# A four-layer network on one NeuronCore: 16-bit one-hots made ahead in two dispatches, and expert sums, latent pieces, layer-norm statistics and a block bias moved in the program

## Chip, cores and metric

The kernel runs on one core of a Trainium2 chip, in one launch. The metric is the device time of that launch in microseconds (us), the median over runs. Five engines run their own instruction lists, each in order: TensorE (PE; its weight loads are listed as PEld), VectorE (DVE), ScalarE (ACT), GpSimd (POOL) and SyncE (SP). They meet through semaphores. Transfers run on 16 DMA engines and are issued from the lists of SP and POOL.

## What is computed

The activations `x` are 4 sequences of 512 tokens with 256 features. Four layers follow one another. Each normalises `x` and adds an attention part and a feed-forward part, both taken from the same normalised rows:

```python
for layer in (L0, L1, L2, L3):
    xn = layernorm(x)
    x = x + layer.attn(xn) + layer.ffn(xn)

L0.attn: gated projection, then a decaying scan over tokens
L0.ffn : "thought" vector of the last token, 4 residual MLP steps, gated broadcast
L1.attn: dilated attention, 16 heads, segments of 64, every 2nd token
L1.ffn : mixture of 32 experts (width 128), each token goes to its best 4
L2.attn: 16 heads of gated linear attention with 64 memory slots:
         ok = read of keys through the slots, pv = softmax(ok), o = read of values,
         o = rms_norm(o) * g * sigmoid(g), then Wo
L2.ffn : x + causal latent attention (16 heads, rotary half), then a mixture of
         7 routed experts (best 2) and one shared expert (width 128)
L3.attn: causal attention, one head of 256
L3.ffn : mixture of 8 experts (width 512), each token goes to its best 2
```

All of it is float32 in the reference.

## The kernel before

**Data.** `x` lies on the chip as 16 tiles of 128 tokens by 256 features; four tiles are one sequence, called a block here (0 to 3). `xn` holds the normalised rows, `xnT` their transpose. A second use of the word block is a group of 128 picked rows of one expert: that is the unit in which the mixtures of experts are computed.

**Mixtures of experts.** The picks of a layer are sorted by expert into slots (`dispatch` in layers 2 and 3 with 38 and 39 blocks of 128 slots; `places1` in layer 1 with 126). TensorE counts the picks (`count`, `rank`, L213 and L215) and VectorE works out each pick's slot. Then comes the inversion, from slot to token: for each of 16 token tiles and each of its picks (2 in `dispatch`, 4 in `places1`) VectorE makes two one-hots, `place` (L268, 128 x 128, which slot inside a block) and `token` (L270, 128 x blocks, the token's number in the column of its block), and TensorE adds their product into `in_slot` (L273). In layer 3 the one-hots lie in a tile called `pieces`, and by that name they stand in the profile. `in_slot` is the index list of the gathers: `load_rows` (L334) issues an indirect DMA from GpSimd for each expert block's rows; L365 transposes them (`rt`), the expert's products follow, and L374 scatters the results to memory. In layer 1 and layer 3 a count that is only known on the chip selects one of several compiled programs (`Switch`), a branch of all engines. `places1` already has 16-bit one-hots (`lane` L1252, `token` L1254, every fourth `token` on GpSimd) in rings of eight buffers.

**Layer 1.** After the branch, `Line` runs the expert blocks as turns of two, with gathers ahead. `block_bias` (`hot` L1293, `bt` L1295, `bb` L1303) makes the bias of every block from a one-hot of its expert. Sums go back through indirect gathers: `collect1` issues for every token tile four gathers (L1277, into tiles that appear as `xn` and `xnT`) and VectorE adds each to `x` with its weight (L523). The layer norm of block 0 that layer 2 begins with follows (`st` L429, `mv` L430, `rs` L418 and L420 on GpSimd, `xn` L448, then the transposes `tr` L463).

**Layer 2.** Work is written as generators, and each `yield` ends a piece; the order in which pieces are drawn is the program order, and a scheduler keeps each engine's list near to it. 32 units (8 for each block, two heads each) of the linear attention are run by `run(u, beside, rate)`. A unit's steps are a string of 19 letters: `m` is this unit's chain, `s` the supply of the next unit's projections, `d` the drain of the unit before. After each step it adds `rate` to a credit, and draws one piece of a beside-chain for each whole credit:

- units 0 to 23: `latent_chain`, 208 pieces at 0.44 a step; what is left is drawn to its end after unit 23. It has its own norm (`junk`, `rms`, `a`), projections (`kp`, `qp`, `vp`), and for each head a pass that finds the maxima (`qk` L2061, `mx` L2068) and one that computes the values (`kq` L2093, `pr` L2098, `pv` L2109). `qk` and `kq` share a pool of four PSUM buffers.
- units 24 to 29: `routed2`, the dispatch and the routed experts, at 1.45 a step;
- unit 30: `ended2` at 0.75: the expert sums (`collect`: two plain loads for each pair of token tiles, a GpSimd addition L390, a VectorE addition to `x` L392), the norm of block 0 for layer 3 and its routing;
- unit 31: `ahead3`, norms and routing of blocks 1 and 2.

In units 0 to 5 the steps with `n % 8 != 7` also draw from `collects`, the layer-1 sums of blocks 1 to 3, five tiles deep. `issue_after` keeps an instruction's place in its engine's list behind a marked one. In the chain of a unit the names that matter are `eF` (L1677, L1678), `turn` (L1698), `ke` (L1720, L1722), `sc`/`s` (L1730, L1736), `pok`/`ok`/`okt` (L1763, L1774, L1778), `pov` (L1809) and `o` (L1858).

**Layer 3.** TensorE's order is written out: groups of `in_slot` products lie between the attention's scores `sc`, the transposes `pt` (L2391), `ov` (L2422) and the output product `o` (L1474). One-hots and their ring of four lie in a weight buffer not yet needed.

Of the kernel before, what the change touches and what calls it, by code (L numbers as in the profile page):

```python
# [14 lines left out]
P = 128  # L15
NB = 4
# [99 lines left out]
class Net:  # L116
    def __init__(self, ctx, tc, a):
# [55 lines left out]
        self.lane = const.tile([P, P], F32, tag="lane", name="lane")  # L173
        nc.gpsimd.iota(self.lane, [[1, P]], base=0, channel_multiplier=0, allow_small_or_imprecise_dtypes=True)
        self.starts = const.tile([P, 96], F32, tag="starts", name="starts")
        nc.gpsimd.iota(self.starts, [[P, 96]], base=0, channel_multiplier=0, allow_small_or_imprecise_dtypes=True)
# [22 lines left out]
    def dispatch(self, moe, rows, top, w, wk, pool, tag, keep=None):  # L199
# [8 lines left out]
        keep = keep or wk  # L208
# [56 lines left out]
        for i in range(NTILE):  # L265
            for m in range(k):
                place = wk.tile([P, P], F32, tag="place", name="place", bufs=4)
                nc.vector.tensor_scalar(place, self.lane, inside[:, i, m : m + 1], None, ALU.is_equal)  # L268
                token = wk.tile([P, blocks], F32, tag="token", name="token", bufs=4)
                nc.vector.tensor_scalar(  # L270
                    token, self.starts[:, :blocks], first[:, i, m : m + 1], less[:, i : i + 1], ALU.is_equal, ALU.mult
                )
                nc.tensor.matmul(  # L273
                    ps, place, token, start=(i == m == 0), stop=(i == NTILE - 1 and m == k - 1)
                )
            if i % 2:
                yield
# [100 lines left out]
    def collect(self, moe, wk, of=range(0, NTILE, 2)):  # L378

        for i in of:  # L380
            x = self.x[:, i : i + 2, :]
            ys = []
            for m in range(moe["k"]):
                y = wk.tile([P, 2, D], F32, tag="sum", name="sum", bufs=8)
                s = (m * NTILE + i) * P
                self.load(y, moe["outs"][s : s + 2 * P, :].rearrange("(n p) d -> p n d", p=P))
                ys.append(y)
            if moe is self.moe2:
                for m in range(len(ys) // 2):
                    self.nc.gpsimd.tensor_tensor(ys[m], ys[m], ys.pop(), ALU.add)  # L390
            for y in ys[1:] + ys[:1]:
                self.nc.vector.tensor_tensor(x, x, y, ALU.add)  # L392
# [434 lines left out]
    def slots1(self, counts, upto, rank, once, go_on, rt):  # L827
# [9 lines left out]
        own = self.starts[:, :ne]  # L837
# [158 lines left out]
    def table1(self, routing):  # L996
# [19 lines left out]
        self.lane16 = routing.tile([P, P], F16, tag="lane16", name="lane16")  # L1016
        nc.gpsimd.tensor_copy(self.lane16, self.lane)
        self.starts16 = routing.tile([P, 126], F16, tag="starts16", name="starts16")
        nc.gpsimd.iota(self.starts16, [[P, 126]], base=0, channel_multiplier=0, allow_small_or_imprecise_dtypes=True)
# [28 lines left out]
    def layer1(self):  # L1048
        nc, a, moe, r1 = self.nc, self.a, self.moe1, self.r1
        with ExitStack() as ctx:  # L1050
# [54 lines left out]
            for pairs in self.arms1(0, [1 + 2 * i for i in range(PAIRS // 2 + 1)]):  # L1105
                line = Line(self)
                self.fetch1(4)
                self.block_bias(bias, wa, ptr, po, (bg, bu1))
# [134 lines left out]
    def places1(self, wk, pool):  # L1243
# [39 lines left out]
    def block_bias(self, bias, wk, ptr, psm, biases):  # L1283
# [9 lines left out]
        nc.vector.tensor_scalar(hot, self.lane[:n, :ne], of, None, ALU.is_equal)  # L1293
# [7 lines left out]
        ps = psm.tile([P, 2, n], F32, tag="o", name="bb")  # L1301
# [179 lines left out]
    def layer2(self):  # L1481
# [8 lines left out]
        with ExitStack() as ctx:  # L1490
# [33 lines left out]
            def run(u, beside, rate):  # L1524
# [18 lines left out]
            collects = {b: self.collect1(b, 5) for b in range(1, NB)}  # L1543
# [21 lines left out]
            run(UNITS - 2, self.ended2(wk, gp["ex"]), 0.75)  # L1565
# [137 lines left out]
    def gated_unit(self, t):  # L1703
# [70 lines left out]
        nc.vector.tensor_tensor(ok, pok, rz, ALU.mult)  # L1774
# [422 lines left out]
    def layer3(self):  # L2197
        nc, a = self.nc, self.a
        with ExitStack() as ctx:
# [9 lines left out]
            with self.tc.manual_schedule(engines={mybir.EngineType.PE}):  # L2209
# [12 lines left out]
                slots = self.dispatch(moe, self.rows, self.top3, self.w3, pieces, psm, "sm", wp)  # L2222
# [304 lines left out]
```

## Time and profile before

| | us |
|---|---|
| median of 3 runs (2184.61, 2185.09, 2187.05) | 2185.09 |
| profiled execution, whole time | 2185.53 |
| its span in the trace | 2183.7 |
| PE busy / share of span | 1960.7 / 90% |
| PEld busy | 1439.0 / 66% |
| DVE busy | 1195.1 / 55% |
| ACT busy | 829.1 / 38% |
| POOL busy | 639.5 / 29% |

The mean granted TensorE clock of the profiled execution is 0.927 of full speed. Line numbers (L268) are those of the kernel before. Where a view gives "idle before" or "waited for", it names the instruction that released the waiting one last. "issue" is a wait that the profile cannot assign. The layers lie about at these places of the span: layers 0 and 1 to about 420 us, layer 2 to about 1830, layer 3 to the end.

### The profile page before, as it was taken

Reading aid. Unit: us, or ns where it says so; the run is one execution under the profiler, and the core shown is the slowest. Engines: PE = TensorE matmul, PEld = TensorE weight load, DVE = VectorE, ACT = ScalarE, POOL = GpSimd, SP = SyncE. Lnnn points to the kernel's source line nnn. Section 1 sums busy time; section 2 is a strip of 40 time slices with the busy share of each in tenths; the row PEclk is TensorE's granted clock in tenths of the full one; section 3 lists DMA queues with packets and bytes.
Section 4 is the critical chain, followed back from the end, with each engine's and each line's share of the span. In section 5 each row is a group of like instructions: output and inputs, shape, how many; then the busy total and the mean of one; then the engine's idle time right before and its main releaser. Section 6 shows DMA issues by size and latency. Waiting matters only on the chain.

```text
span 2183.7 us, 35377 instructions
## 1 busy us (share of the span) xinstructions
PE 1960.7 (90%) x13015; PEld 1439.0 (66%) x13015; DVE 1195.1 (55%) x3451; ACT 829.1 (38%) x1678; POOL 639.5 (29%) x746
## 2 busy tenths in 40 slices
PE   5854998488999999999999999999999979799995
PEld 2522877255666766667666676667787867578895
DVE  5747674486656565555565555546556564413222
ACT  1253344323344443334443343342445434335321
POOL 6334572563211211111211211111454451022231
PEclk9955999678999999999999999987999989899998
DMA  8412885621000000000000000101433220267796
GB/s 289 136 38 82 282 271 155 183 61 32 1 1 9 23 10 6 1 1 8 22 11 6 1 1 8 42 11 47 151 120 111 82 80 1 69 219 263 232 329 234
DMA packets 149549, 198.21 MB, mean 91 GB/s; under 512 B 16885, under 2 KB 127576, under 8 KB 149208
## 3 DMA queue, kind: packets, MB, share of 16 engines
q1 hardware_dynamic: 135224, 156.40, 22.0%
q0 software_dynamic: 14112, 39.15, 6.0%
q8 instruction: 111, 1.82, 0.3%
q14 instruction: 102, 0.84, 0.1%
HBM read 154.21 MB, written 41.29 MB: 90 GB/s over the span
## 4 chain that ended last, share of the span: by engine, by line
PE 56%; DVE 9%; issue 6%; POOL 5%; DMA 4%; ACT 2%; SPq 0%; DVEq 0%; POOLq 0%; ACTq 0%
PE pt L1745 8%; PE pj L1667 6%; PE o L1858 4%; PE g L2278 4%; PE kq L2093 3%; PE sc L1730 3%; PE pov L1809 2%; DVE junk L2068 2%; PE pv L2109 2%; PE qk L2061 2%; PE o L2291 2%; DMA r<-l_rows,in_slot 1%; PE st L1718 1%; PE turn L1698 1%; PE pok L1763 1%
## 5 line engine op out<-in xcount | busy, mean ns | idle before, releaser
L2068 DVE CUSTOM_DVE_ANT_0 junk<-qk,hide 128x512 f32<-128x512 f32 (+3 forms) x256 | 124.5, 486 | 43.6 <-PE qk L2061 25.1
L2101 POOL TENSOR_SCALAR_AFFINE_SELECT pr<-pr 128x512 f32<-128x512 f32 x64 | 40.3, 642 | 341.3 <-ACT pr L2098 341.3
L2278 PEld LDWEIGHTS g<-rT,we 128*128 128x128 f32 x1120 | 132.0, 194 | 5.3 <-ACT rT L367 3.3
L2278 PE MATMUL g<-rT,we 128*128 128x128 f32 x1120 | 132.9, 278 | 1.8 <-ACT rT L367 1.8
L1745 PE MATMUL pt<-Wg,xnT 128*128 128x256 f32 x512 | 126.2, 399 | 2.0 <-ACT h L1630 1.0
L334 POOL DMA_INDIRECT r<-l_rows,in_slot x73 | 72.2, 989 | 189.4 <-PE rt L365 104.9
L374 POOL DMA_INDIRECT l_outs<-y,to x73 | 72.5, 993 | 182.0 <-ACT y L373 148.0
L1745 PE MATMUL pt<-Wv,xnT 128*128 128x256 f32 x512 | 122.4, 391 | 0.0
L1858 PE MATMUL o<-Wo,oT 128*128 128x256 f32 x512 | 122.0, 381 | 0.0
L1736 DVE TENSOR_TENSOR s<-sc,keep 128x512 f32<-128x512 f32 x128 | 82.4, 683 | 67.2 <-PE sc L1730 67.1
L1680 DVE RECIPROCAL rz<-rz 128x128 f32<-128x128 f32 x128 | 116.8, 933 | 0.4
L1745 PEld LDWEIGHTS pt<-Wg,xnT 128*128 128x128 f32 x512 | 98.2, 198 | 27.3 <-issue 6.5
L346 DVE TENSOR_TENSOR mine<-r,number 128x2 f32<-128x2 f32 x73 | 12.8, 175 | 177.0 <-DMA r<-l_rows,in_slot 169.5
L1745 PEld LDWEIGHTS pt<-Wv,xnT 128*128 128x128 f32 x512 | 96.5, 194 | 15.7 <-issue 0.2
L2098 ACT ACTIVATE pr<-kq 128x512 f32<-128x512 f32 (+1 forms) x192 | 86.1, 530 | 48.5 <-PE kq L2093 48.1
L1858 PEld LDWEIGHTS o<-Wo,oT 128*128 128x128 f32 x512 | 96.2, 197 | 8.5 <-issue 0.7
L1313 POOL DMA_INDIRECT r<-l_rows,in_slot x84 | 83.2, 990 | 61.9 <-PE rt L1325 28.1
L2093 PE MATMUL kq<-q,kT 32*128 32x128 f32 (+3 forms) x512 | 87.4, 490 | 7.6 <-DVE mx L2068 5.9
L1748 ACT COPY v<-pt 128x512 f32<-128x512 f32 x64 | 37.5, 586 | 129.2 <-PE pt L1745 129.2
L1826 DVE TENSOR_TENSOR o<-pov,g 128x512 f32<-128x512 f32 x64 | 41.3, 686 | 77.0 <-ACT sq L1825 77.0
L1831 POOL TENSOR_TENSOR rs<-ms,sm 128x8 f32<-128x8 f32 x32 | 6.6, 205 | 243.0 <-DVE ms L1829 242.9
L1825 ACT ACTIVATE sq<-pov 128x512 f32<-128x512 f32 x64 | 34.8, 595 | 102.6 <-PE pov L1815 77.4
(561 smaller groups left out, 4624.2 us busy)
## 6 DMA issues: line engine op xcount, KB each, us to landing
we<-l_w SPq DMA_DIRECT2D x70, 512.0 KB
we<-l_wo SPq DMA_DIRECT2D x35, 512.0 KB
l_outs<-none SPq DMA_DIRECT2D x1, 11776.0 KB
l_outs<-y SPq DMA_DIRECT2D x42, 256.0 KB
we<-l_r_gate SPq DMA_DIRECT2D x38, 128.0 KB
we<-l_r_up SPq DMA_DIRECT2D x38, 128.0 KB
we<-l_r_down SPq DMA_DIRECT2D x38, 128.0 KB
l_rows<-xn SPq DMA_DIRECT2D x8, 544.0 KB
```

Of the source, the lines that this page charges most:

```text
L334: self.nc.gpsimd.indirect_dma_start(out=r[:, m, :], out_offset=None, in_=moe["rows"][:, :], in_offset=bass.IndirectOffsetOnAxis(ap=moe["in ...
L374: self.no_order(moe["name"] + " back", nc.gpsimd.indirect_dma_start(out=moe["outs"][:, :], out_offset=bass.IndirectOffsetOnAxis(ap=to, axi ...
L1313: nc.gpsimd.indirect_dma_start(out=r[:, i, :], out_offset=None, in_=moe["rows"][:, :], in_offset=bass.IndirectOffsetOnAxis(ap=moe["in_slot ...
L1667: nc.tensor.matmul(ps, w[n][:, k, :], self.xnT[:, k, t["b"] * T : (t["b"] + 1) * T], start=(k == 0), stop=(k == KD - 1))
L1680: inverse = lambda c: nc.vector.reciprocal(rz[:, c * P : (c + 1) * P], rz[:, c * P : (c + 1) * P])
L1736: nc.vector.tensor_tensor(s, ps[hh], keep4, ALU.mult)
L1745: nc.tensor.matmul(ps[:, i, :], self.xnT[:, k, s : s + P], w[n][:, k, :], start=(k == 0), stop=(k == KD - 1))
L1858: nc.tensor.matmul(ps[:, p, :], of_parity(oT[:, h, c * D : (c + 1) * D], p), wo[:, h, :], start=(h == 0), stop=(h == 1),)
L2068: nc.vector.tensor_tensor_reduce(out=junk[:, :m], in0=tiles[j][:, off : off + m], in1=self.hide[:, T - m :], op0=ALU.add, op1=ALU.max, sca ...
L2093: nc.tensor.matmul(tiles[j][:, BLOCK[i] - off : BLOCK[i] - off + T - i * P], kT[r, i * P : (i + 1) * P], qT[r, i * P :], start=True, stop= ...
L2098: nc.scalar.activation(pr[:, j, off : off + m], tiles[j][:, :m], AF.Exp, scale=0.25)
L2278: nc.tensor.matmul(pt[:, m, :], we[:, q, k * T + m * P : k * T + (m + 1) * P], rT[:, k, :], start=(k == 0), stop=(k == KD - 1),)
```

## The change

- In `dispatch` the one-hots and the two rows of numbers that they are compared with become 16-bit (`lane16`, `starts16`); the one-hots lie in rings of eight; a tile's products are put two tiles behind its one-hots. In layer 3 the one-hots come from the pool `wk3` (`hots`). `places1` has rings of 12 instead of 8. Layer 1's own uses of the float32 rows get small tiles `own` and `lane32`.
- `block_bias` is called after the second turn instead of before the first, with its two small products in the pool `pd`.
- The statistics of block 0's layer norm are spread between the layer-1 sums, a tile's after the tile's last sum, instead of after all.
- Unit 0 of layer 2 begins with a credit of -8 steps; gathers of later blocks are drawn only after its sixth step, eight tiles deep instead of five.
- `collect` is split into `fetch_rows` (loads) and `add_rows` (additions). `ended2` issues the loads of the first four pairs at once, yields six times, and puts the additions behind `ok` of the unit (`self.late`); its credit is 1.0 a step instead of 0.75.

```diff
@@ -262,17 +262,22 @@
         nc.vector.tensor_tensor(inside, slots, first, ALU.subtract)
         nc.vector.tensor_scalar(less, self.number[:, :NTILE], float(-NB * T), None, ALU.add)
         ps = pool.tile([P, blocks], F32, tag=tag, name="in_slot")
-        for i in range(NTILE):
-            for m in range(k):
-                place = wk.tile([P, P], F32, tag="place", name="place", bufs=4)
-                nc.vector.tensor_scalar(place, self.lane, inside[:, i, m : m + 1], None, ALU.is_equal)
-                token = wk.tile([P, blocks], F32, tag="token", name="token", bufs=4)
-                nc.vector.tensor_scalar(
-                    token, self.starts[:, :blocks], first[:, i, m : m + 1], less[:, i : i + 1], ALU.is_equal, ALU.mult
-                )
-                nc.tensor.matmul(
-                    ps, place, token, start=(i == m == 0), stop=(i == NTILE - 1 and m == k - 1)
-                )
+        ones = []
+        for i in range(NTILE + 2):
+            if i < NTILE:
+                for m in range(k):
+                    place = hots.tile([P, P], F16, tag="place", name="place", bufs=8)
+                    nc.vector.tensor_scalar(place, self.lane16, inside[:, i, m : m + 1], None, ALU.is_equal)
+                    token = hots.tile([P, blocks], F16, tag="token", name="token", bufs=8)
+                    nc.vector.tensor_scalar(
+                        token, self.starts16[:, :blocks], first[:, i, m : m + 1], less[:, i : i + 1], ALU.is_equal, ALU.mult
+                    )
+                    ones.append((place, token))
+            if i > 1:
+                for m in range(k):
+                    nc.tensor.matmul(
+                        ps, *ones[(i - 2) * k + m], start=(i == 2 and m == 0), stop=(i == NTILE + 1 and m == k - 1)
+                    )
             if i % 2:
                 yield
         moe["in_slot"] = in_slot = tile("in_slot", P, blocks, dt=mybir.dt.uint32, of=keep)
...
@@ -378,18 +383,24 @@
     def collect(self, moe, wk, of=range(0, NTILE, 2)):
 
         for i in of:
-            x = self.x[:, i : i + 2, :]
-            ys = []
-            for m in range(moe["k"]):
-                y = wk.tile([P, 2, D], F32, tag="sum", name="sum", bufs=8)
-                s = (m * NTILE + i) * P
-                self.load(y, moe["outs"][s : s + 2 * P, :].rearrange("(n p) d -> p n d", p=P))
-                ys.append(y)
-            if moe is self.moe2:
-                for m in range(len(ys) // 2):
-                    self.nc.gpsimd.tensor_tensor(ys[m], ys[m], ys.pop(), ALU.add)
-            for y in ys[1:] + ys[:1]:
-                self.nc.vector.tensor_tensor(x, x, y, ALU.add)
+            self.add_rows(moe, i, self.fetch_rows(moe, i, wk))
+
+    def fetch_rows(self, moe, i, wk):
+        ys = []
+        for m in range(moe["k"]):
+            y = wk.tile([P, 2, D], F32, tag="sum", name="sum", bufs=8)
+            s = (m * NTILE + i) * P
+            self.load(y, moe["outs"][s : s + 2 * P, :].rearrange("(n p) d -> p n d", p=P))
+            ys.append(y)
+        return ys
+
+    def add_rows(self, moe, i, ys):
+        x = self.x[:, i : i + 2, :]
+        if moe is self.moe2:
+            for m in range(len(ys) // 2):
+                self.nc.gpsimd.tensor_tensor(ys[m], ys[m], ys.pop(), ALU.add)
+        for y in ys[1:] + ys[:1]:
+            self.nc.vector.tensor_tensor(x, x, y, ALU.add)
 
 
 
...
@@ -1105,7 +1116,6 @@
             for pairs in self.arms1(0, [1 + 2 * i for i in range(PAIRS // 2 + 1)]):
                 line = Line(self)
                 self.fetch1(4)
-                self.block_bias(bias, wa, ptr, po, (bg, bu1))
                 at = lambda n: 2 * n if n < STATIC // 2 + pairs else None
                 pieces = self.beside1(bd, wa, ptr, pd, [dilated(u) for u in (2, 3, 4, 5)])
                 credit, rate = 0.0, 35 / (STATIC // 2 + pairs - 1)
...
@@ -1113,6 +1123,8 @@
                     line.turn(
                         dict(t=2 * n, n=n, parts=[static(2 * n), static(2 * n + 1)], done=static_done), at(n + 3)
                     )
+                    if n == 1:
+                        self.block_bias(bias, wa, ptr, pd, (bg, bu1))
                     if n in (8, 10):
                         self.fetch1(singles_at + n - 8, held[n // 2 - 4])
                     credit += rate
...
@@ -1152,10 +1164,20 @@
             last = [dilated(u) for u in (6, 7)]
             next(last[0])
             turns = {1: 0, 4: 0, 5: 1, 8: 1, 10: 0, 12: 1}
+            st, mv = self.stats.tile([P, 4, 6], F32, tag="st", name="st"), self.stats.tile([P, 4, 2], F32, tag="mv", name="mv")
             for n, _ in enumerate(self.collect1(0, 2)):
+                if n > 4 and n % 4 == 1:
+                    i = n // 4 - 1
+                    nc.vector.bn_stats(st[:, i, :], self.x[:, i, :])
+                    nc.vector.bn_aggr(mv[:, i, :], st[:, i, :])
                 if n in turns:
                     next(last[turns[n]])
-            self.layer_norm(0)
+            rs = self.stats.tile([P, 4], F32, tag="rs", name="rs")
+            self.rsqrt(rs, mv[:, :, 1], 1.0, 1e-5)
+            for i in range(4):
+                nc.vector.tensor_scalar(
+                    self.xn[:, i, :], self.x[:, i, :], mv[:, i, 0:1], rs[:, i : i + 1], ALU.subtract, ALU.mult
+                )
             for chain in last:
                 for _ in chain:
                     pass
...
@@ -1248,9 +1270,9 @@
         ps = pool.tile([P, blocks], F32, tag="o", name="in_slot")
         for i in range(NTILE):
             for m in range(4):
-                lane = wk.tile([P, P], F16, tag="lane", name="lane", bufs=8)
+                lane = wk.tile([P, P], F16, tag="lane", name="lane", bufs=12)
                 nc.vector.tensor_scalar(lane, self.lane16, inside[:, i, m : m + 1], None, ALU.is_equal)
-                token = wk.tile([P, blocks], F16, tag="token", name="token", bufs=8)
+                token = wk.tile([P, blocks], F16, tag="token", name="token", bufs=12)
                 (nc.gpsimd if m == 3 else nc.vector).tensor_scalar(
                     token, self.starts16[:, :blocks], first[:, i, m : m + 1], self.less[:, i : i + 1], ALU.is_equal,
                     ALU.mult,
...
@@ -1298,7 +1320,7 @@
         bT = wk.tile([ne, 3, P], F32, tag="bT", name="bT", bufs=1)
         nc.vector.tensor_copy(bT[:, 0, :n], pt[:ne, 0, :n])
         nc.vector.tensor_copy(bT[:, 1:, :], pt[:ne, 1:3, :])
-        ps = psm.tile([P, 2, n], F32, tag="o", name="bb")
+        ps = psm.tile([P, 2, n], F32, tag="d", name="bb")
         for m in range(2):
             nc.tensor.matmul(ps[:, m, :], bT[:, 1 + m, :], bT[:, 0, :n], start=True, stop=True)
         nc.vector.tensor_copy(bias, ps)
...
@@ -1527,11 +1549,11 @@
                 supply = supplies(u + 1) if u + 1 < UNITS else iter(())
                 gathered = collects.get(u // 2 + 1, iter(())) if u < 6 else iter(())
                 drain = self.gated_drain(units[u - 1]) if u else iter(())
-                credit = 0.0
+                credit = 0.0 if u else -8 * rate
                 chains = {"m": self.gated_unit(units[u]), "s": supply, "d": drain}
                 for n, what in enumerate("mmmmsmsmmdmmsmsdmsd" if u + 1 < UNITS else "mmmmdmmdmmdmmm"):
                     next(chains[what], None)
-                    if n % 8 != 7:
+                    if n % 8 != 7 and (u or n > 5):
                         with self.tc.issue_after(marks[min(u // 2, NB - 1)]):
                             next(gathered, None)
                     credit += rate
...
@@ -1540,7 +1562,7 @@
                         next(beside, None)
 
             marks = []
-            collects = {b: self.collect1(b, 5) for b in range(1, NB)}
+            collects = {b: self.collect1(b, 8) for b in range(1, NB)}
             norms = [normed(b) for b in range(NB)]
             for it in (norms[0], supplied(0)):
                 for _ in it:
...
@@ -1562,7 +1584,7 @@
                 run(u, routed, 1.45)
             for _ in routed:
                 pass
-            run(UNITS - 2, self.ended2(wk, gp["ex"]), 0.75)
+            run(UNITS - 2, self.ended2(wk, gp["ex"]), 1.0)
             run(UNITS - 1, self.ahead3(gp["ex"]), 1.0)
             drain = self.gated_drain(units[UNITS - 1])
             for chain in (self.units3[0], self.units3[0], drain, self.units3[0], drain, drain):
...
@@ -1571,8 +1593,14 @@
 
     def ended2(self, wk, pool):
 
+        rows = {i: self.fetch_rows(self.moe2, i, wk) for i in range(0, 8, 2)}
+        for _ in range(6):
+            yield
         for i in range(0, NTILE, 2):
-            self.collect(self.moe2, wk, (i,))
+            with self.tc.issue_after(self.late):
+                self.add_rows(self.moe2, i, rows[i])
+            if i + 8 < NTILE:
+                rows[i + 8] = self.fetch_rows(self.moe2, i + 8, wk)
             yield
             if i == 2:
                 self.layer_norm3(0)
...
@@ -1771,7 +1799,7 @@
                     start=False, stop=True, skip_group_check=True,
                 )
         ok = wk.tile([P, T], F32, tag="ok", name="ok")
-        nc.vector.tensor_tensor(ok, pok, rz, ALU.mult)
+        self.late = nc.vector.tensor_tensor(ok, pok, rz, ALU.mult).ins
         yield
         pt = pp.tile([P, 8, 64], F32, tag="ps", name="okt")
         for c in range(4):
...
@@ -2219,7 +2247,7 @@
                 next(units[1])
                 pieces = self.wexp.tile([P, 3, 4, D], F32, tag="we", name="pieces")
                 pieces = Ring(pieces.rearrange("p q e d -> p (q e d)"), None)
-                slots = self.dispatch(moe, self.rows, self.top3, self.w3, pieces, psm, "sm", wp)
+                slots = self.dispatch(moe, self.rows, self.top3, self.w3, pieces, psm, "sm", wp, self.wk3)
 
                 def slots_on():
                     with self.tc.high_priority():
```

More of the change, by code (lines that the diff above doesn't have):

```diff
@@ L170, in __init__ @@
         nc.gpsimd.iota(self.number, [[P, 96]], base=0, channel_multiplier=1, allow_small_or_imprecise_dtypes=True)
[L173 to L176, printed above, removed]
+        self.lane16 = const.tile([P, P], F16, tag="lane16", name="lane16")
+        nc.gpsimd.iota(self.lane16, [[1, P]], base=0, channel_multiplier=0, allow_small_or_imprecise_dtypes=True)
+        self.starts16 = const.tile([P, 126], F16, tag="starts16", name="starts16")
+        nc.gpsimd.iota(self.starts16, [[P, 126]], base=0, channel_multiplier=0, allow_small_or_imprecise_dtypes=True)
         self.less = const.tile([P, NTILE], F32, tag="less", name="less")
@@ L197, in expert_rows, with dispatch @@
         )
-    def dispatch(self, moe, rows, top, w, wk, pool, tag, keep=None):
+    def dispatch(self, moe, rows, top, w, wk, pool, tag, keep=None, hots=None):
         nc = self.nc
@@ L207, in dispatch @@
         tile = lambda name, *shape, dt=F32, of=wk: of.tile(list(shape), dt, tag=name, name=name, bufs=1)
-        keep = keep or wk
+        keep, hots = keep or wk, hots or wk
         flat = lambda t: t.rearrange("p a b -> p (a b)")
@@ L836, in slots1 @@
         per_tile = lambda t: t.unsqueeze(1).to_broadcast([P, NTILE, ne])
-        own = self.starts[:, :ne]
+        own = self.own
         place, moved, again, beyond = (by_tiles(t) for t in once[:4])
@@ L1015, in table1 @@
         )
[L1016 to L1019, printed above, removed]
+        self.own = tile("own", P, 32)
+        nc.gpsimd.iota(self.own, [[P, 32]], base=0, channel_multiplier=0, allow_small_or_imprecise_dtypes=True)
+        self.lane32 = tile("lane32", P, 32)
+        nc.gpsimd.iota(self.lane32, [[1, 32]], base=0, channel_multiplier=0, allow_small_or_imprecise_dtypes=True)
         self.row128 = routing.tile([P, 1], F32, tag="row128", name="row128")
@@ L1292, in block_bias @@
         nc.vector.tensor_copy(moe["expert"], of)
-        nc.vector.tensor_scalar(hot, self.lane[:n, :ne], of, None, ALU.is_equal)
+        nc.vector.tensor_scalar(hot, self.lane32[:n, :ne], of, None, ALU.is_equal)
         pt = ptr.tile([P, 3, P], F32, tag="tr", name="bt")
```

## The prediction, made before the changed kernel was run

> **What bounds the kernel now.** I read the page's busy times first (TensorE, "PE", is busy for 1960.7 of 2183.7 us, 90%), then the stretches of the span, because an average hides the stages. These are the columns: span, PE, PEld, DVE, ACT and POOL busy, granted clock, DMA share, GB/s.
>
> ```profile
> 400.00:530.00 130.00, 95.78 (x533) 60.01 (x536) 96.59 (x234) 36.06 (x80) 77.30 (x81) 0.76 0.31 91
> 530.00:1500.00 970.00, 954.95 (x6581) 649.25 (x6576) 543.15 (x1302) 383.68 (x720) 163.25 (x191) 0.97 0.03 9
> 1500.00:1530.00 30.00, 29.09 (x154) 24.31 (x153) 26.98 (x125) 6.55 (x11) 3.19 (x4) 0.77 0.30 99
> ...
> 1745.00:1830.00 85.00, 70.93 (x454) 55.30 (x453) 49.03 (x154) 30.98 (x58) 36.18 (x44) 0.89 0.16 52
> 1830.00:1910.00 80.00, 67.48 (x293) 48.52 (x291) 37.74 (x191) 30.12 (x77) 7.55 (x13) 0.90 0.14 46
> ```
>
> From 530 to 1500 TensorE idles 15 of 970 us, and no move of work on other engines can win there. The idle time that the change can reach is at 400 to 530 (34.2 us), 1745 to 1830 (14.1) and 1830 to 1910 (12.5). The stretch 1500 to 1530 looks busy, but not with work that needs the time, as the chain shows below. TensorE's own waits (us in total, times, longest) name the stalls:
>
> ```profile
> PE tr L463 <- DVE xn L448: 22.0, 2, 14.1
> ...
> PE okt L1778 <- DVE ok L1774: 8.9, 2, 4.6
> PE turn L1698 <- ACT eF L1678: 7.8, 1, 7.8
> PE qk L2061 <- DVE mx L2068: 7.1, 3, 5.8
> PE pv L1442 <- ACT e L1433: 7.1, 3, 2.9
> PE bt L1295 <- DVE hot L1293: 6.9, 1, 6.9
> PE pt L2391 <- ACT s L2411: 6.0, 2, 4.0
> ...
> PE rt L1325 <- issue: 5.8, 1, 5.8
> ```
>
> Restricted to 400 to 530, tr waits 7.9, turn 7.8, qk 7.1 and one okt 4.3 us: 27.1 of the 34.2. The other okt (4.6) lies at 1754 to 1758. Then the one-hots of the two later dispatches, line by line, and the chain at the second:
>
> ```profile
> L268 DVE TENSOR_SCALAR place<-lane,inside x32: 268/274/327, 1509.4 to 1522.0; 128x128 f32<-128x128 f32 x32
> L268 DVE TENSOR_SCALAR pieces<-lane,pieces x32: 276/280/289, 1857.8 to 1898.2; 128x128 f32<-128x128 f32 x32
> its engine sat idle before it (us, times) until:
>   PE in_slot L273: 13.4, 4
> ```
> ```profile
> 1510.33 13.26 PE in_slot L273 x62
> ```
>
> In layer 2's dispatch 31 pairs pass in 13.26 us, 0.41 each, at VectorE's pace. In layer 3's it is the reverse: VectorE waits 13.4 us, since four buffers tie it to TensorE's order:
>
> ```profile
> 1886.17 10.62 PE L2422 MATMUL ov<-pT,v 128*128 128x512 f32 x32
> 1896.63 2.53 PE L273 MATMUL in_slot<-pieces 128*128 128x39 f32 x16
> 1898.99 7.16 PE L1474 MATMUL o<-both,oT 128*128 128x256 f32 x32
> 1907.04 1.07 PE L463 MATMUL tr<-ident,both 128*128 128x128 f32 x8 [0.89 <-issue]
> ```
>
> **The base.** The profiled execution took 2185.53 us for a span of 2183.7; the median of the three runs is 2185.09. They agree within 0.5 us, so changes are taken off 2185.5. What can be told from no change is about 0.2%, 4.4 us.
>
> **Layer 1's dispatch and bias (176 to 222): nothing.** VectorE waits 4.0 us, twice, for TensorE to free one of eight one-hot buffers; twelve let it run four pairs further (lane 0.242 and three quarters of the tokens at 0.299, some 0.45 us a pair), at most 4 x 0.45 = 1.8, against a wait of 2.67 and of 1.32: -1.5 (0 to -2.7). The block bias now comes after two turns' gate and up products. The 6.9 us at bt shrink little, because the other branch shows 5.8 us of "issue" before its first rt with no hot in front: about 1 us of the 6.9 is the hot's own. Instead the vector work of bias (hot, bT) stands behind the first blocks' gating, and bb and rt behind it: +1.5 (0 to +3). Sum 0, -2.7 to +3.
>
> **Statistics between the gathers (395 to 425): -2.5.** GpSimd issues 16 gathers at a pitch of 1.26 us; after the last sum (ended 418.5) four statistics pairs run to 420.7, 2.2 us. Only one pair, 0.55, remains: -1.65. The other part is `both` L1949, 2.61 us at 414.28 beside a GpSimd memset (414.78 to 416.61), where its sibling L1947 of the same shape takes 0.48; it now stands ahead of the memset, and the last sums no longer queue behind it: -0.85 of the 2.1, since the last gather has to land as well. Bounds -1.65 and -3.8.
>
> The Trainium skill's GPSIMD Engine Reference (Specifications) says that GpSimd shares its SBUF interfaces with VectorE and contends with operations that have two SBUF inputs; that speaks against more vector work among gathers. The row: the 16 gathers take 0.94 to 0.95 us each whether a two-input sum (0.48) runs beside them or not; the memset beside L1949 shows the stretch, the gathers do not. Were the rule right for gathers too and each statistics pair lengthened one, this part would be an estimated 0.5 us worse for each pair.
>
> **First unit of layer 2 (422 to 530): -5.1.** The chain's latent pieces start 8 steps' credit later (8 x 0.44 = 3.5 pieces), and gathers of later blocks are held back for 6 steps and prefetched 8 deep instead of 5. On GpSimd one gather fewer (1.26) stands before the latent norm's rms and its power; on VectorE two products `a` fewer stand before eF: eF's wait of 7.8 loses 2.5 (bounds 0 and 5). The wait of okt for ok, 4.3, and that of qk for mx, 7.1, come from VectorE work queued behind sums that wait for gathers; both leave the place. What is late next: ke and one xnT copy of unit 1 now stand on VectorE behind block 2's norm and block 3's first sums, and these wait for the rest of the deeper ring: 7 x 1.26 = 8.8. Sum -2.5 - 4.3 - 7.1 + 8.8 = -5.1. If the new wait is covered by latent pieces, -13.9; if qk waits again behind the moved gathers, +2. The row nearest to the new wait is the gathers' pitch, so I keep it whole.
>
> **Layer 2's body (530 to 1500): +3.** Three pieces fewer are paid by credit (197 of 208 before unit 24, from 200), and 11 instead of 8 are flushed after it. There the scores kq and qk share four PSUM buffers and nothing lies between: a qk wait is 2.4 us on average (7.1 over 3), a kq wait 0.5 (5.9 over 12). Three pieces at one us each: +3, from 0 (covered) to +6 (two each).
>
> **Layer 2's dispatch (1499 to 1530): -2.7.** By layer 1's 16-bit row a one-hot of 128x128 takes 0.242 instead of 0.274; for both of a pair, 0.36 for 0.41, over 32 pairs -1.6. TensorE's list now puts sc, turn, four o and half of pov (2.1 + 1.1 + 1.0 + about 0.6 = 4.8 us) ahead of or among the in_slot products, where it had nothing; these used to follow. Against that VectorE takes three reciprocals (0.93 each) and an s (0.68), 3.5 us, before the last one-hots. With -1.6 - 4.8 + 3.5 = -2.9, less 0.2 for the later first one-hot. Bounds: -6.4 (reciprocals hidden) and +1.9 (TensorE's work not saved).
>
> **Sums of expert rows in three units (1745 to 1805): -2.5.** `ok` no longer queues behind sums whose load (1749.19 to 1752.13) and GpSimd addition (1.27 to 1.45) come first: the 4.6 us go. But GpSimd now does the eight additions before block 0's rs and loads 12 and 14 wait for earlier sums, so tr of block 0 and with it sc come late: I replay sc of unit 31 at 1776.7 against 1777.6, block 1's norm 7 us later, and okt of the last unit 1802.3 against 1804.78. Bounds -5 (4.6 and a little kept) and +4 (norm of block 1 ends last).
>
> **Layer 3's dispatch (1851 to 1910): +1.** The products are one 16-bit matmul each instead of two float32 ones (11.5 us for 64 with their waits of 1.0 three times): with 9 of layer 1's in 1.13 us, 32 take 4.0. But TensorE's list puts the last four pairs behind the 16 products `o` (7.2 us), where they stood before it. So in_slot, the overflow count and the branch no longer lie beside `o`. Start of ov: three groups that took 3.7 us take 1.0 each, -8, of which pt's waits for s (6.0) give back most; I take -4. Then ov 10.6, eight pairs 1.0 (from 2.5), o 7.2, four pairs 0.5: in_slot ends at 1886.2 - 4 + 10.6 + 1.0 + 7.2 + 0.5 = 1901.5 against 1899.2, 2.3 later, of which the arm's first gather, requested 5.2 after the count and now with TensorE already done, takes less: +1 (bounds -3 to +5; the uncovered branch is the 5.8 row).
>
> **Sum.** 0 - 2.5 - 5.1 + 3 - 2.7 - 2.5 + 1 = -8.8: 2185.5 - 8.8 = 2176.7.
>
> **Rivals.** *Only the later dispatches and sums gain* (2180 to 2189; 2184): the gathers end block 1's norm whatever stands in front, so the 27.1 us merely change names, and flush and branch eat the -5.2 of the others. For: GpSimd is busy 77.3 of 130 us there, and gathers are paced by it. Against: ok and mx do not need the gathers' data.
>
> *Slower, through VectorE's order* (2190 to 2197; 2193): the deeper ring makes VectorE stand in front of two rings, block 2's and block 3's, instead of part of one; the second costs 8 x 1.26 + 3.0 for the landing (422.34 to 425.30) = 13.1, and qk's 7.1 stays. Then -8.8 + 13.1 + 3.6 (half of qk's) = +8. It decides if more than one ring's waiting lands before unit 2's okt. For: VectorE is as busy as TensorE there (96.6). Against: PE has latent pieces to run.
>
> *Larger* (2160 to 2168; 2165): the new wait of 8.8 and the 3 of the flush are both covered.
>
> **Numbers.** Forecast 0.59 (2169 to 2181), first rival 0.18, slower 0.15, larger 0.08. The range 2165 to 2191 leaves out some of the slower and half of the larger. Faster by over 0.2%: 0.59 + 0.08 = 0.67, and 0.01 of the first rival: 0.68; same 0.17; slower 0.15.
>
> **What would show it.** Right: the place rows at about 0.24 in f16; no VectorE wait for in_slot; in 400 to 530 at least 5 us less TensorE idle and ke or xnT named as the new wait; okt out of the list at 1754; in_slot of layer 3 ended after `o`. Wrong: the 400 to 530 idle unchanged, the flush after unit 23 over 6 us longer, or tr of the first expert of layer 3 more than 4 us behind.

## The result: 0.6% slower, and the profile after

The changed kernel takes 2198.34 us (median of 7 runs, 2193.7 to 2209.86), the kernel before in the same runs and those shown above 2186.61 (7 runs, 2182.01 to 2190.19). The ratio is 1.0063, 95% interval 1.0041 to 1.0086, so the slowdown is small but beyond the noise. The profiled execution after took 2197.15 us, span 2195.3, clock 0.922; it is 11.6 us longer than the one before. 2176.7 was forecast, and the time lies above the range.

TensorE's waits of the changed kernel show the named stalls gone or smaller: okt does not wait more than 0.3 us anywhere, and from 400 to 530 us the longest waits are these (us in total, times, longest):

```profile
PE sc L1452 <- ACT q L1439: 8.8, 4, 4.8
PE turn L1726 <- ACT eF L1706: 5.9, 1, 5.9
PE tr L474 <- DVE xn L1178: 5.0, 1, 5.0
PE pj L1695 <- issue: 3.8, 1, 3.8
PE sc L1758 <- DVE o L1854: 3.5, 1, 3.5
```

(L1178 is the norm's last step that stood at L448, L1706 the eF of L1678, L1452 layer 1's attention.) The layer norm waits 5.0 instead of 7.9, eF 5.9 instead of 7.8, and qk, further down that list, 2.5 instead of 7.1. So where are the 11.6 us? I cut the span at products that both kernels have: the first transposition of block 0's norm, `okt` of units 2, 22 and 23, the second dispatch's `count`, `okt` of unit 31. First the rows before, then those after, each with its ends, span, PE, PEld, DVE, ACT and POOL busy, granted clock, DMA share, GB/s:

```profile
422.65:562.71 140.06, 119.77 (x670) 75.54 (x670) 98.14 (x242) 40.20 (x85) 68.58 (x73) 0.84 0.19 57
562.71:1377.99 815.28, 807.76 (x5615) 553.22 (x5611) 472.18 (x1108) 323.84 (x605) 137.57 (x156) 0.99 0.03 9
1377.99:1419.61 41.62, 40.83 (x297) 26.81 (x293) 21.95 (x54) 16.80 (x32) 6.39 (x8) 0.96 0.07 20
1419.61:1499.43 79.82, 73.61 (x435) 47.60 (x431) 32.50 (x95) 31.33 (x62) 12.89 (x19) 0.85 0.03 8
1499.43:1804.63 305.20, 285.70 (x1957) 233.27 (x1956) 188.30 (x640) 128.65 (x262) 129.98 (x138) 0.94 0.34 106
```
```profile
424.69:561.73 137.04, 120.11 (x618) 73.82 (x618) 92.72 (x232) 37.11 (x78) 67.98 (x70) 0.83 0.19 58
561.73:1386.77 825.04, 815.38 (x5633) 558.76 (x5632) 469.67 (x1104) 329.35 (x615) 137.98 (x158) 0.98 0.03 8
1386.77:1426.01 39.24, 39.24 (x279) 25.99 (x275) 24.68 (x64) 15.12 (x26) 7.02 (x8) 1.00 0.14 45
1426.01:1515.74 89.73, 84.94 (x487) 55.81 (x483) 34.44 (x100) 33.72 (x67) 13.69 (x20) 0.79 0.03 7
1515.74:1815.42 299.68, 278.07 (x1917) 223.46 (x1916) 184.91 (x629) 126.45 (x260) 128.76 (x137) 0.95 0.35 108
```

Before these: +2.0. Then -3.0, +9.8, -2.4, +9.9, -5.5, and +0.8 behind `okt` 31: 11.6 us. The loss lies in units 3 to 22 and in the flush after unit 23, where the change moved nothing by hand, except that unit 0 had drawn fewer latent pieces. In units 3 to 22 TensorE's idle time hardly grew (span less busy time: 7.5 us before, 9.7 after), but its busy time did, by 7.6 us for 18 products more of 5615. The clock records of the two traces show a difference: TensorE ran at half speed for 20.5 us of this stretch before, for 34.1 after. In the flush it is 23.9 and 37.5 us.

### The profile page after: what moved, and what is told of

Its sections match the earlier page's. It is cut to its first block, busy times and chain, and to the rows that moved or that the text cites. A ratio compares the mean times of both kernels' runs of the same rounds, so it can differ in the third digit from the quotient of the medians.

```text
span 2195.3 us, 35251 instructions
## 1 busy us (share of the span) xinstructions
PE 1964.9 (90%) x12951; PEld 1434.6 (65%) x12951; DVE 1188.3 (54%) x3448; ACT 830.8 (38%) x1680; POOL 638.8 (29%) x746
## 4 chain that ended last, share of the span: by engine, by line
PE 57%; DVE 8%; issue 6%; POOL 5%; DMA 4%; ACT 2%; SPq 0%; another core or an unknown queue 0%; POOLq 0%; DVEq 0%; ACTq 0%
PE pt L1773 8%; PE pj L1695 6%; PE o L1886 5%; PE g L2306 3%; PE kq L2121 3%; PE sc L1758 3%; PE pov L1837 3%; PE qk L2089 2%; PE pv L2137 2%; PE o L2319 2%; DMA r<-l_rows,in_slot 1%; PE turn L1726 1%; DVE junk L2096 1%; PE st L1746 1%; PE pov L1843 1%
## 5 line engine op out<-in xcount | busy, mean ns | idle before, releaser
L1773 PE MATMUL pt<-Wg,xnT 128*128 128x256 f32 x512 | 130.7, 408 | 3.0 <-DVE pv L1812 1.3
L2121 PE MATMUL kq<-q,kT 32*128 32x256 f32 (+3 forms) x512 | 93.6, 500 | 8.4 <-DVE mx L2096 7.1
L2121 PEld LDWEIGHTS kq<-q,kT 32*128 32x128 f32 x512 | 44.6, 196 | 51.2 <-DVE mx L2096 32.7
```

The source lines that it names most:

```text
L1773: nc.tensor.matmul(ps[:, i, :], self.xnT[:, k, s : s + P], w[n][:, k, :], start=(k == 0), stop=(k == KD - 1))
L2121: nc.tensor.matmul(tiles[j][:, BLOCK[i] - off : BLOCK[i] - off + T - i * P], kT[r, i * P : (i + 1) * P], qT[r, i * P :], start=True, stop= ...
```

## The experiments

The theories. **Flush:** more latent pieces after unit 23 (drawn there to the chain's end: the flush) cost more than their work, because TensorE has little else there. **Phase:** eight pieces are drawn in every unit, so a kind of piece meets particular steps of a unit; a shift by four puts it beside others, and the body (units 3 to 22) pays. Rivals: the deeper ring of gathers, or layer 1. (A count of the draws corrects a number of the prediction: the credit restarts at every unit, so eight pieces a unit are drawn and not 8.36. 16 pieces, not 8, are flushed before, and 20, not 11, after.) All ratios are to the kernel before, run on the same chip, with 95% intervals.

**Without unit 0's credit.**
```diff
-                credit = 0.0 if u else -8 * rate
+                credit = 0.0
```


> The changed kernel, but unit 0 of layer 2 begins with a credit of 0 again, so 16 latent pieces instead of 20 are left to be drawn after unit 23. Theory A (the flush: after unit 23 TensorE has little but 32-row scores, its granted clock falls to a half, and four more pieces there cost 8 to 10 us; from the last unit before the flush to the second dispatch the changed kernel is 8.4 us longer): about 9 us faster than the changed kernel, 0.2% above the kernel before. Theory B (the deeper ring of gathers holds VectorE in units 1 and 2): no difference from the changed kernel (0.6% above before). Theory C (the bias moved in layer 1 and the branch there, 3 to 4.6 us, and the later dispatch): no difference from the changed kernel either.

0.9976 (0.9961 to 0.9991). The one line is worth 0.9% (1.0063 against 0.9976), some 19 us and twice what theory A gave the flush; B and C forecast nothing. Its `okt` 2 to `okt` 22 takes 817.5 us, 2.2 more than the kernel before. The profiles of this version and the next three, beside which the kernel before took 2204.5 us, reach block 0's norm 15 to 21 us later than its first one did (443.4 instead of 422.65 in the one that has its program up to there), so stages are compared from the norm on.

**Without the gathers' edit.**
```diff
-                    if n % 8 != 7 and (u or n > 5):
+                    if n % 8 != 7:
...
-            collects = {b: self.collect1(b, 8) for b in range(1, NB)}
+            collects = {b: self.collect1(b, 5) for b in range(1, NB)}
```


> The changed kernel, but the gathers of layer 1's sums in units 0 to 5 are drawn as before (from the first step, five tiles deep). Theory A (flush): no difference from the changed kernel, 0.6% above before; the early stalls only decide in which unit latent pieces fall. Theory B (ring of gathers): the 8 to 10 us that unit 2 is longer are gone, within 0.2% of the kernel before. Theory C: as A.

1.0047 (1.0029 to 1.0064): as slow as the changed kernel within the intervals, against theory B. The ring is not the cause.

**No flush, in the changed kernel and in the one before.**
```diff
-        first, beside = 24, 0.44
+        first, beside = 24, 0.48
```


> The changed kernel with 0.48 latent pieces a step instead of 0.44, so nine a unit instead of eight and none left after unit 23. Theory A: the flush of 20 pieces (some 45 us of which 37 at half clock) lies beside the units' own products at full clock: 12 to 18 us faster than the changed kernel, 0.1 to 0.3% below the kernel before. Theory B and C: the pieces only change their place, within 3 us of the changed kernel (0.5 to 0.7% above before).

> The kernel before with 0.48 latent pieces a step instead of 0.44: none of the 16 left after unit 23. Theory A: 8 to 14 us faster than the kernel before (ratio 0.994 to 0.996), since 24 us of half clock lie there. Theory B and C: within 0.1% of the kernel before.

1.0109 (1.0087 to 1.0131) and 1.0095 (1.0059 to 1.0131): both slower, against every theory. In the second, the stretch from unit 23's `okt` to unit 24's falls by 43 us (81.1 to 38.1), as the flush theory had it, but from `okt` 2 to `okt` 23 64 us are added. So the theory's remedy was wrong. Why nine pieces a unit cost that much in the body no run parts further; 44.4 us at half speed there, for 20.5, are a part of it.

**Phase and flush apart.** Four versions with the same four pieces at other places; only the credit that a unit begins with is changed:
```diff
-                credit = 0.0 if u else -8 * rate
+                credit = (0.0 if u else -8 * rate) + {1: 4.0}.get(u, 0)    # back in unit 1
+                credit = (0.0 if u else -8 * rate) + {23: 4.0}.get(u, 0)   # back in unit 23
+                credit = 0.0 + {23: -4.0}.get(u, 0)                        # flush alone
```
```diff
-                credit = 0.0
+                credit = 0.0 + {23: 4.0}.get(u, 0)                         # before, flush of 12
```


> The changed kernel; the four latent pieces that unit 0 does not draw (it draws 4 instead of 8) are drawn at unit 1's first step, so unit 2 and all later ones begin at the same piece as in the kernel before, and 16 pieces are left after unit 23. Theory P (phase: eight pieces a unit meet the same steps of a unit in every unit, and a shift by four pieces puts them beside other steps, at a cost in the body) and theory F (flush: four more pieces after unit 23 cost 8 to 13 us): both give the ratio of the version without the credit, 0.996 to 0.999 of the kernel before. Above 1.004: neither, the cost is in units 0 to 2.

> The changed kernel; the four pieces are drawn at the first step of unit 23: units 1 to 22 are shifted by four pieces as in the changed kernel, 16 pieces are left for the flush. Theory F: 8 to 13 us faster than the changed kernel, ratio to the kernel before 0.998 to 1.002. Theory P: the shift stays, so within 4 us of the changed kernel, 1.004 to 1.007.

> The changed kernel with unit 0's credit at 0, and with four pieces fewer in unit 23: no shift in units 0 to 22, 20 pieces after unit 23. Theory F: as slow as the changed kernel, 1.003 to 1.008 of the kernel before. Theory P: the flush has room, at most 3 us over the version without the credit, 0.996 to 0.999.

> The kernel before with four pieces more in unit 23 and so 12 instead of 16 after it. Theory F: 6 to 10 us faster than the kernel before (0.995 to 0.997). Theory P: nothing (0.999 to 1.001). Theory S (each piece that is added to a unit of eight costs more there than in the flush, as the denser rate of 0.48 showed): slower, 1.001 to 1.004.

Back in unit 1: 1.0000 (0.9983 to 1.0017). Back in unit 23: 1.0047 (1.0027 to 1.0068). Flush alone: 0.9998 (0.9980 to 1.0016). Before with a flush of 12: 0.9958 (0.9942 to 0.9975). The three versions of the changed kernel and the one without the credit form a square:

| | 16 flushed | 20 flushed |
|---|---|---|
| body in phase | 0.9976 | 0.9998 |
| body shifted by four | 1.0047 | 1.0063 |

Down the columns the shift costs 0.71 and 0.65%, some 14 to 16 us, beyond the intervals, and theory F alone is rejected: the flush alone was to be 1.003 or more. In the left column not all of it is the body's: four pieces are also moved there from unit 0 to unit 23, which takes 52.4 us with them, against 40.0. Along the rows four pieces in the flush cost 0.22 and 0.16%, some 3.5 to 5 us, which the intervals (about 0.2% to either side) do not part from nothing. Back in unit 1 is slower than both theories gave (0.996 to 0.999): the four extra pieces take their time there (147.5 us from the norm to `okt` 2, against 140.1 in the flush-alone version and 142.2 without the credit). The kernel before with a flush of 12 gains 0.42%, as theory F forecast and against theory P. So the flush is dear, but it is the smaller part of this loss.

**The shift alone, by four and by eight, in the kernel before.**
```diff
-                credit = 0.0
+                credit = 0.0 + {2: -4.0, 23: 4.0}.get(u, 0)   # by four
+                credit = 0.0 + {2: -8.0, 23: 8.0}.get(u, 0)   # by eight
```


> The kernel before, where unit 2 draws four latent pieces fewer (4 instead of 8) and unit 23 four more (12): the pieces of units 3 to 22 are shifted by four, the flush stays at 16 pieces, and nothing else of the change is in it. Theory P (phase): 12 to 18 us slower than the kernel before, 1.005 to 1.008, with a longer stretch from unit 2's to unit 23's okt and more half-speed clock in it. Theory F (flush alone): no difference (0.999 to 1.001).

> The kernel before, where unit 2 draws none and unit 23 sixteen: a shift by eight pieces, a whole unit's worth, so that each piece from unit 3 on meets the same step as before, one unit later. Theory P: units 3 to 22 take the times of units 2 to 21 before; what is lost is only in units 2 and 23 (sixteen pieces in one unit, up to 10 us): 1.000 to 1.005. Theory D (any delay of the latent chain costs, in proportion): twice the shift by four, 1.009 to 1.014.

By four: 1.0055 (1.0034 to 1.0077). From `okt` 2 to `okt` 22 it takes 826.3 us instead of 815.3, as the changed kernel does (825.0), with 41.0 us at half speed; four more pieces in unit 23 take it to 54.1 us from 41.6. By eight: 1.0046 (1.0028 to 1.0064), at the upper end of what phase allowed and far from twice the shift by four. The two times are not told apart, but the traces are. The shift by eight takes 811.2 us from `okt` 2 to `okt` 22, of which unit 3 has 33.4 instead of 41.1, since unit 2's pieces are missing there; from `okt` 3 on it takes 777.8 us, the kernel before 774.1, the shift by four 786.1. And the late units repeat the kernel before one unit later: units 13 to 18 take 40.35, 44.04, 46.52, 42.00, 39.24, 38.20 us, its units 12 to 17 took 40.35, 44.06, 46.52, 41.68, 39.24, 38.20 (among the earlier ones up to 3 us differ, both ways). What it loses is unit 23, 63.9 instead of 41.6 us for sixteen pieces. So a delay alone is not what costs in the body; a delay by half a unit is.

The units' times also show what half a unit does here, and it is not quite what theory P says. The 208 latent pieces are 52 for each of the four sequences, six and a half units of eight. So in every version neighbouring sequences stand half a unit apart, and the kernel before has both phases itself: the changed kernel's units 4 to 10 draw the same kinds of pieces as its units 10 to 16 (the same counts of `kq`, `qk` and `lg` products in each), and those are its slow units. Sums of unit times, in us:

| units | before | changed kernel | before, shifted by four |
|---|---|---|---|
| 3 to 9 | 282.5 | 295.6 | 289.6 |
| 10 to 16 | 292.9 | 280.0 | 281.6 |
| 17 to 22 | 239.8 | 249.4 | 255.0 |

Over 13 units, two whole sequences, the two kernels take nearly the same (units 4 to 16: 534.3 and 534.6 us; 10 to 22: 532.8 and 529.4). The shift by four exchanges the phases of the sequences, and the +9.8 us are +13.1 - 12.9 + 9.5: units 3 to 22 now hold two slow stretches and one fast one instead of one and two.

**The rest of the change, and a combination.**
```diff
-                credit = 0.0 if u else -8 * rate
+                credit = 0.0
...
-                    if n % 8 != 7 and (u or n > 5):
+                    if n % 8 != 7:
...
-            collects = {b: self.collect1(b, 8) for b in range(1, NB)}
+            collects = {b: self.collect1(b, 5) for b in range(1, NB)}
```


> The changed kernel without the edits of unit 0 (credit 0, gathers from the first step, five deep): dispatch, sums, bias and statistics alone. The prediction gave these -2.7, -2.5, 0, -2.5 and +1 = -6.7 us: ratio 0.997 (0.995 to 0.999). If the gathers' edit is worth what the prediction gave the okt and qk waits, the version with it but without the credit (0.9976) is 3 us or more faster than this; if it is worth nothing, they are equal.

0.9976 (0.9959 to 0.9993): 5 us faster than the kernel before; dispatch, sums, bias and statistics together do what was forecast, within the interval. It equals the version with the gathers' edit and without the credit: the gathers' edit is worth nothing that can be told.

```diff
-                credit = 0.0 if u else -8 * rate
+                credit = 0.0 + {23: 4.0}.get(u, 0)
```


> The changed kernel with unit 0's credit at 0 and four pieces more in unit 23, so 12 after it: the version without the credit (0.9976) together with the shorter flush (0.9958 alone). If the two add: 0.9934 (0.991 to 0.996) of the kernel before, faster than both kernels. If the flush's gain needs the old order after it: 0.997 to 0.999.

0.9952 (0.9938 to 0.9967): 2178.79 us against 2188.67, faster than both kernels. It is not told apart from the kernel before with a flush of 12 alone (0.9958), and lies at the edge of the range for adding (0.9934 is just below its interval), so whether the two gains add in full stays open.

## Why the prediction was wrong

**The step that failed is the body's.** "Three pieces at one us each: +3" for 530 to 1500 priced the pieces' number (which was four, not three) and not their place, and it left the body at zero. Measured: +9.8 in units 3 to 22, -2.4 in unit 23, +9.9 in the flush, 17.3 together. Of the 9.9, 4.7 also stand in the flush-alone version, which draws the same 20 pieces there (84.5 us, 23.9 at half speed); the other 5.2 come with the 13.6 us more at half speed. The stretch was read as safe because TensorE idled only 15 of 970 us there. But a stretch without idle time still has a speed, and here it differs with what stands beside what. In the changed kernel's timeline (start, duration) unit 7 has the 32-row scores (`kq`) at a place where TensorE has few other products:

```profile
725.59 1.09 PE L1879 MATMUL ot<-ident,o 128*128 128x128 f32 x8
728.31 1.13 PE L2121 MATMUL kq<-q,kT 32*128 32x384 f32 x4 [1.63 <-DVE mx L2096]
729.37 0.70 PE L1773 MATMUL pt<-Wg,xnT 128*128 128x256 f32 x2
730.20 3.55 PE L2121 MATMUL kq<-q,kT 32*128 32x384 f32 x12
733.67 5.39 PE L1773 MATMUL pt<-Wg,xnT 128*128 128x256 f32 x14
```

From 731.1 to 738.0 the clock is granted at half, and the 14 products of pt take 5.39 us. The kernel before has the same rows, but in unit 13, with the clock at half from 971.5 to 981.7:

```profile
970.76 1.37 PE L2093 MATMUL kq<-q,kT 32*128 32x384 f32 x4 [1.64 <-DVE mx L2068]
972.07 1.22 PE L1745 MATMUL pt<-Wg,xnT 128*128 128x256 f32 x2
973.22 2.98 PE L2093 MATMUL kq<-q,kT 32*128 32x384 f32 x12
976.13 6.05 PE L1745 MATMUL pt<-Wg,xnT 128*128 128x256 f32 x14
```

In unit 7 of the version without the credit, whose phases are those of the kernel before, the value products pv stand ahead of pt, and 16 take 3.72:

```profile
743.22 1.09 PE L1879 MATMUL ot<-ident,o 128*128 128x128 f32 x8
744.25 2.36 PE L2137 MATMUL pv<-pr,both 128*32 128x512 f32 x32
746.54 3.72 PE L1773 MATMUL pt<-Wg,xnT 128*128 128x256 f32 x16
```

At half the clock half is done, so by estimate 13.6 us more of it are worth up to 6.8 us, and TensorE idles 2.1 us more: up to 8.9 of the 9.8 us. The other traces agree: between `okt` 2 and `okt` 22 the seven versions with the old phases take 813.3 to 818.7 us with 17.1 to 30.7 at half speed, the four that are shifted by four 825.0 to 827.3 with 34.1 to 41.0. That scores in a run lower the clock is read from where the half-speed stretches start; no run set the mix of products alone. And only half of the 13.6 us stands beside scores (23.9 us instead of 17.1); the rest follows `lg` products (10.2 instead of 3.4), of which the last section tells.

**Unit 0: -5.1 forecast, -3.0 measured, and not for the reasons given.** The waits for ok and mx went, but ok's also went where unit 0's edits are taken back (1.2 us or less), and eF's is 5.6 us there; only mx's returns (6.3 us in all). And the versions that draw unit 0's pieces as before take as long from the norm to `okt` 2 as the kernel before (140.1 and 142.2 us in two profiles with the gathers' edit, 139.8 without it, against 140.1). The -3.0 is the work of four pieces that was put off. The okt and qk terms, -11.4, were not worth their waits: new ones (sc for o 3.5, pj 3.8, and layer 1's sc 8.8 instead of 3.4) took their place. The signs set for this part failed too: from 400 to 530 us TensorE idles 31.4 us instead of 34.2, not 5 less, and neither ke nor xnT is named as a new wait.

**Right within their bounds.** *Layer 1:* forecast 0. From the first `in_slot` product to the first output product it loses 0.3 us; bt's wait fell from 6.9 to 2.4, and rt waits 5.6 for its gathers instead. The second branch's "issue" before rt is 8.7 instead of 5.8, but it is 5.2 in the changed kernel without unit 0's edits and 8.6 in the kernel before with a flush of 12, which up to there are the changed kernel and the kernel before: it varies from execution to execution. *Statistics:* from the first rt after that branch to the norm's tr -2.5, as forecast; the VectorE step that took 2.61 us beside GpSimd's memset takes 0.48, though its sibling now takes 1.17 there. *Layer 2's dispatch:* -4.3 from `count` to unit 29's `okt`, forecast -2.7. The first rt comes 3.4 us later, not earlier, and the units around it are shorter: so the gain fits work that now stands ahead; no run takes this edit alone. *Sums:* -1.2 to unit 31's `okt`, forecast -2.5; the two sum to -5.5 against -5.2. *Layer 3's dispatch:* from `count` to the first `g` -1.1, forecast +1. VectorE still waits for TensorE, now for the ring of eight:

```profile
L270 DVE TENSOR_SCALAR place<-lane,inside x32: 246/248/250, 1528.6 to 1539.8; 128x128 f16<-128x128 f16 x32
L270 DVE TENSOR_SCALAR place<-lane,pieces x32: 244/247/254, 1869.0 to 1903.3; 128x128 f16<-128x128 f16 x32
...
its engine sat idle before it (us, times) until:
  PE in_slot L278: 9.2, 2
```

The 16-bit place takes 0.247 us for 0.274 to 0.280, as forecast, and "no VectorE wait for in_slot" was wrong: 9.2 us instead of 13.4. The branch lies open behind `o`, as feared, and TensorE waits 7.0 us there; ov's earlier start pays for it (6.0 us earlier after `count`, forecast 4):

```profile
1902.15 7.16 PE L1496 MATMUL o<-both,oT 128*128 128x256 f32 x32
1909.15 0.26 PE L278 MATMUL in_slot<-token,place 128*128 128x39 f16 x4
1916.40 2.06 PE L474 MATMUL tr<-ident,both 128*128 128x128 f32 x8 [7.00 <-ACT both L2389]
```

**The rivals.** The slower one named VectorE behind two rings of gathers; the runs without that edit reject it. The sign was its sign, the mechanism another, and 2198.3 lies above even its range, so that it came nearest is luck. "The flush over 6 us longer" was among the marks of a wrong forecast, and it came: 9.9.

## What to carry to other kernels

Where one chain is drawn in a fixed number of pieces beside another, the number of pieces that come early or late is not the price of a move: their place beside the other chain counts. Work out first how long the chain's own period is in units; here a sequence is six and a half, so both phases stand in both kernels, and a shift by half a unit cost some 0.7%, most of it because one more slow stretch came to lie in the body. After any edit to how many are drawn, put the same unit of both kernels side by side and see whether it takes the same time; a shift by a whole unit gave most units their old times back. Then compare a whole period, since a slower unit may be an old one that came earlier. And where an engine has no idle time, look at its clock before calling the stretch safe.

## What the runs showed of the hardware

TensorE's granted clock falls to a half inside a stretch that is busy to 99%. In the changed kernel four of the seven half-speed stretches between 560 and 1430 us follow a window of 3.4 us in which most products are 32-row scores (9 of 11, 14 of 14, 14 of 16 and 6 of 8, with 0.4 to 1.0 us idle). Before the other three there are none of these, but 22 to 24 `lg` products (a routing product, 7 columns wide) and no idle time. The stretches last 3.4 us or a multiple. Under the shift by four they add up to 41.0 us between `okt` 2 and `okt` 22 against 20.5 us in the kernel before.

In all 14 traces every change of the granted clock lies on one grid of 3.413 us from the trace's first. Where a string of the 24 `lg` products (3.5 us) starts on this grid goes with what follows it. Between `okt` 2 and `okt` 22 of the twelve traces that draw eight pieces a unit there are 36 such strings: the 26 that started within 0.5 us behind a grid point, or 1.9 us and more behind it, were followed by half speed, and the ten that started 1.2 to 1.7 us behind one were not. So a part of the time at half speed changes with where a product happens to fall, whatever the phase.
